# Perceiver block: the context product of batches 2 to 14 as seven half products instead of eight

## The chip, the core and the metric

One Trainium2 chip, one core. The time is the device time of one execution of the kernel, in microseconds (us). The engines are TensorE (PE in the profile; its weight loads are PEld), VectorE (DVE), ScalarE (ACT), GpSimd (POOL) and SyncE (SP, which only issues DMAs here). All tensors are float32.

## The reference

Sixteen batches of 128 tokens with 512 features pass through three layers. Only the first is touched by the change:

```python
def _L0_xattn_ref(hidden_states, visual_hidden_state):
    scores = jnp.einsum('bld,bvd->blv', hidden_states, visual_hidden_state)
    probs = jax.nn.softmax(scores, axis=-1)
    return jnp.einsum('blv,bvd->bld', probs, visual_hidden_state)
...
x = x + _L0_xattn_ref(_layernorm(x, axis=-1), ctx_1024)
x = x + _L0_attn_ref(_layernorm(x, axis=-1), ...)
x = x + _L0_ffn_ref(_layernorm(x, axis=-1), ...)
```

`ctx_1024` holds 2048 rows of 512 features for each batch. The "context product" is the second einsum: 128 x 2048 weights times 2048 x 512 context rows. The second layer is causal self-attention with 16 heads of 32 (its query, key and value weights are two factors, multiplied out once at the start), the third picks 2 of 8 low-rank experts for each batch.

## The kernel before

**Tiling.** A batch is 128 tokens on 128 partitions, or its transpose. The context is handled in four quarters of 512 rows (`v` = 0 to 3); the quarter comes twice from memory, once transposed (`ctxT`, for the scores) and once as rows (`ctx`, for the product), 1 MB each, four buffers each. `score` computes one quarter's scores, transposed, with 16 matmuls of 128x128x128 into a PSUM bank `psc`; `keep_score` copies them into the tile `sc` (ScalarE) and keeps a running maximum `mx` (VectorE). `turn_max`, `most`, `spread` turn that maximum into one value per token, spread over all partitions. `less` subtracts it (VectorE, one 128x512 instruction for each quarter), `power` takes the exponential (ScalarE), `sums` adds up the 16 tiles of the batch (VectorE). `attend` is the context product of one quarter: four matmuls with 128 weights columns and 512 moving columns, all 16 of the batch accumulating in one PSUM bank `av`. `x1_of` divides by the sum and adds the residual in one VectorE instruction that reads `av` from PSUM, and starts the next layer norm (`moments`: two VectorE instructions, then the reciprocal root `rs` as two small GpSimd instructions; `rows`: the normalized rows `h`; `turn`: a 32x32 transposition on VectorE and two DMAs through memory that give `hT`).

**One iteration of the main loop** (`b` = 0 to 13) works on four batches at once: self-attention of batch `b`, softmax and context product of `a = b + 1`, scores of `s = b + 2`, and the expert layer of `l = b - 1`. On TensorE its order is: tr_m (the transposed maximum of `a`), q, spread, k, v (projections of `b`), attend(a,0), compare (the 16 heads' scores `pss`), attend(a,1), lg (the expert logits), attend(a,2), den (the sum of the weights), attend(a,3), score(s,0), mid (experts, first factor), score(s,1), score(s,2), ffn (experts, second factor), y (the heads times v, from `pT`), score(s,3), o (the product with Wc). `mid` is written with 64 columns of the array for each of the two experts, side by side; `y` with 32 columns for each of four heads, `compare` with 32 rows for each of four heads.

VectorE in the same iteration: nm, diag (for `spread`), x2 and its norm, the four `less`, `h` and `turn` of layer 3, rotation of q and k (`rotate`: a shuffle, a product with the cosines; GpSimd does the product with the sines; `rotated` adds the two), `sums`, the router's `shares`, four groups of mask and maximum (`powers`), the choice of experts (`choose`), x1 and its norm, ten transpositions of 32 rows into `pT` (`turn_probs`), and the maxima `mx` of the next scores. GpSimd: `rs` of each norm, the token order for v, the residual of layer 3, the two products with the sines, four divisions of the probabilities (`divided`), three indirect DMAs (`fetch`), and the output's DMA.

**What sets the order.** Every instruction is issued through a wrapper that keeps the program order on its engine, so each engine works through a list written out by hand, and waits where an input or a buffer isn't there. Tiles come from pools with a fixed number of buffers in turn (`p1`: 1, `p2`: 2, `p3`: 3, `p4`: 4); a new tile waits until the reader of the one it replaces is done. The eight PSUM banks: 2 for scores (`ps_sc`), 1 for the context product (`ps_av`), 5 for all else (`ps_acc`). The DMAs of SP stand in one list too.

After the loop, batches 14 and 15 are finished by a list of their own; in it GpSimd adds up the sums of batch 15. In the profile nearly every instruction carries line 101, that of the wrapper, so rows are told apart by their tiles.

Of the kernel before, what the change touches and what calls it, by code (L numbers as in the profile page):

```python
# [11 lines left out]
F32 = mybir.dt.float32  # L12
# [3 lines left out]
ALU = mybir.AluOpType  # L16
# [50 lines left out]
def perceiver_block(ctx: ExitStack, tc: tile.TileContext, io: dict, out: bass.AP):  # L67
# [5 lines left out]
    p3 = ctx.enter_context(tc.tile_pool(name="p3", bufs=3))  # L73
    p4 = ctx.enter_context(tc.tile_pool(name="p4", bufs=4))
    ps_sc = ctx.enter_context(tc.tile_pool(name="ps_sc", bufs=2, space=PSUM))
    ps_av = ctx.enter_context(tc.tile_pool(name="ps_av", bufs=1, space=PSUM))
    ps_acc = ctx.enter_context(tc.tile_pool(name="ps_acc", bufs=5, space=PSUM))

    dram = ctx.enter_context(tc.tile_pool(name="dram", bufs=2, space=bass.MemoryType.DRAM))

# [25 lines left out]
    def bank(of, tag, name):  # L106
        return of.tile([P, 512], F32, tag=tag, name=name)
# [124 lines left out]
            cts[b, v] = t  # L232

    norms, hTs = {}, {}
    scs, mxs, psc, parts, dens, rdens, avs, spreads, trs = ({} for _ in range(9))
    x1s, x2s, projected, partners, turned_qk, values, hTvs = ({} for _ in range(7))
    atts, ys, yTs, os_, routes, mids, ffns = ({} for _ in range(7))
# [19 lines left out]

    def keep_score(b, v):
        if v == 0:
            scs[b] = p2.tile([P, VC, 4, S], F32, tag="sc", name=f"sc_{b}")  # L260
            mxs[b] = p1.tile([P, 4, S], F32, tag="mx", name=f"mx_{b}")
        sc, mx, ps = scs[b], mxs[b], psc.pop((b, v))
        act.copy(sc[:, v], ps)
        if v:
            dve.tensor_tensor(mx, ps, mx if v > 1 else sc[:, 0], ALU.max)
        if v == VC - 1:
            dve.tensor_tensor(mx[:, :2], mx[:, :2], mx[:, 2:], ALU.max)
            dve.tensor_tensor(mx[:, 0], mx[:, 0], mx[:, 1], ALU.max)
# [20 lines left out]
    def less(b, v):  # L289
        sc = scs[b]  # L290
        dve.tensor_tensor(
            sc[:, v], sc[:, v], spreads[b][:, None, :S].to_broadcast([P, 4, S]), ALU.add
        )

    def power(b, v):
        act.activation(scs[b][:, v], scs[b][:, v], AF.Exp)

    def sums(b, by=dve):
        sc = scs[b]
        t = p1.tile([P, 4, S], F32, tag="sums", name=f"sums_{b}")  # L300
        for v in range(1, VC):
            by.tensor_tensor(t, sc[:, v], t if v > 1 else sc[:, 0], ALU.add)
        part = p2.tile([P, S], F32, tag="part", name=f"part_{b}")
        by.tensor_tensor(t[:, :2], t[:, :2], t[:, 2:], ALU.add)
        by.tensor_tensor(part, t[:, 0], t[:, 1], ALU.add)
        parts[b] = part

    def attend(b, v):
        sc, ct = scs[b], cts.pop((b, v))
        if v == 0:  # L310
            avs[b] = bank(ps_av, "av", f"av_{b}")
        for j in range(4):
            matmul(
                avs[b], sc[:, v, j, :], ct[:, j, :],
                start=(v == 0 and j == 0), stop=(v == VC - 1 and j == 3),
            )
# [7 lines left out]
        dve.reciprocal(rdens[b], dens.pop(b)[:, :1])  # L324

    def x1_of(b):
        x1s[b] = p2.tile([P, D], F32, tag="x1", name=f"x1_{b}")
        dve.scalar_tensor_tensor(x1s[b], avs.pop(b), rdens.pop(b), xs.pop(b), ALU.mult, ALU.add)
        norms[2, b] = Norm(x1s[b], f"2_{b}", mixed=b in (0, B - 1), hT=(p1, "hT2")).moments()


# [12 lines left out]

    def rotate(b, n, by=pool):
        ps = projected.pop((n, b))
        partner = p1.tile([P, HC, S], F32, tag=f"{n}P", name=f"{n}P_{b}")
        dve.stream_shuffle(partner.rearrange("p c t -> p (c t)"), ps, PARTNERS)
        t = p1.tile([P, HC, S], F32, tag=f"{n}T", name=f"{n}T_{b}")
        dve.tensor_tensor(  # L350
            t, ps.rearrange("p (c t) -> p c t", c=HC),
            cst[:, None, C_COS : C_COS + S].to_broadcast([P, HC, S]), ALU.mult,
        )
        by.tensor_tensor(
            partner, partner, cst[:, None, C_SIN : C_SIN + S].to_broadcast([P, HC, S]), ALU.mult
        )
        turned_qk[n, b], partners[n, b] = t, partner
# [17 lines left out]
        projected["v", b] = ps  # L375

    def keep_v(b):
        values[b] = p2.tile([P, D], F32, tag="vv", name=f"vv_{b}")
        act.copy(values[b], projected.pop(("v", b)))

    def compare(b):
        qT, kT = turned_qk.pop(("q", b)), turned_qk.pop(("k", b))
        pss = [bank(ps_acc, "acc", f"pss_{b}_{j}") for j in range(4)]
        for c in range(HC):
            for j, ps in enumerate(pss):
                of = slice(j * DH, (j + 1) * DH)
                matmul(
                    ps[:, c * S : (c + 1) * S], qT[of, c, :], kT[of, c, :], start=True, stop=True
                )
        atts[b] = (  # L390
            p1.tile([P, H, S], F32, tag="att", name=f"att_{b}"),
            p2.tile([P, H], F32, tag="nmx", name=f"nmx_{b}"),
            p2.tile([P, H], F32, tag="sm", name=f"sm_{b}"),
            p2.tile([P, H], F32, tag="rsm", name=f"rsm_{b}"),
            pss,
        )
# [119 lines left out]
    def fetch(b):  # L516
        blocks, picked, ex = chosen[b]
        spare = b == B - 1
        each = (p2 if spare else p1).tile(
            [P, TOP, KC * R], F32, tag="sc" if spare else "each", name=f"each_{b}"  # L520
        )
        for i in range(TOP):
            pool.indirect_dma_start(
                each[:, i, :], None, io["A"],
                bass.IndirectOffsetOnAxis(ap=blocks[:, i : i + 1], axis=0),
            )
        wb = p2.tile([P, D], F32, tag="wb", name=f"wb_{b}")
        pool.indirect_dma_start(
            wb, None, io["BT"], bass.IndirectOffsetOnAxis(ap=picked, axis=0)
        )  # L530
        routes[b] = each, wb
# [26 lines left out]
    def first_joined(b):  # L558
        acc, v0 = bank(ps_acc, "acc", f"o0_{b}"), state["v0"]
        for c in range(KC):  # L560
            matmul(acc[:1, :], v0[:, c : c + 1], w["c"][:, c, :], start=(c == 0), stop=(c == KC - 1))
        row = p1.tile([1, D], F32, tag="sums", name=f"row_{b}")
        dve.tensor_tensor(row, acc[:1, :], x1s[b][:1, :], ALU.add)
        state["h"] = Norm(row, f"row_{b}", 1, "mx", mixed=True).moments()

# [128 lines left out]
    for b in range(B - 2):  # L694
        l, a, s = b - 1, b + 1, b + 2
        if b:
            turn_max(a)
            project(b, "q", [0])
            most(a)
            x2_of(l)  # L700
            spread(a)
            project(b, "q", [1, 2, 3])
            order_tokens(b)
            less(a, 0)
            power(a, 0)
            rows(3, l)
            turn(3, l)
            less(a, 1)
            power(a, 1)
            residual(l)  # L710
            load_x(s + 1)
            load_turned(s, 2)
            less(a, 2)
            power(a, 2)
        else:
            project(b, "q")
        rotate(b, "q")
        project(b, "k")
        if b:
            less(a, 3)  # L720
            power(a, 3)
            load_turned(s, 3)
        rotated(b, "q")
        rotate(b, "k")
        project_v(b)
        keep_v(b)
        rotated(b, "k")
        attend(a, 0)
        load_ctx(a + 1, 0)
        compare(b)  # L730
        if b:
            sums(a)
            shares(l)
        powers(b, 0)
        attend(a, 1)
        load_ctx(a + 1, 1)
        powers(b, 1)
        if b:
            logit(l)
            choose(l)  # L740
        divided(b, 0)
        if b:
            fetch(l)
        attend(a, 2)
        powers(b, 2)
        divided(b, 1)
        whole(a)
        portion(a)
        powers(b, 3)
        divided(b, 2)  # L750
        if b:
            gate(l)
        load_ctx(a + 1, 2)
        attend(a, 3)
        divided(b, 3)
        x1_of(a)
        score(s, 0)
        turn_probs(b, 0)
        rows(2, a)
        turn(2, a)  # L760
        keep_score(s, 0)
        if b:
            middle(l)
        for i in (1, 2):
            turn_probs(b, i)
        score(s, 1)
        turn_probs(b, 3)
        keep_score(s, 1)
        load_ctx(a + 1, 3)
        score(s, 2)  # L770
        if b:
            widen(l)
            end(l)
        load_turned(s + 1, 0)
        heads(b)
        keep_heads(b)
        keep_score(s, 2)
        score(s, 3)
        if s + 1 < B:
            norm1(s + 1)  # L780
        load_turned(s + 1, 1)
        if s + 1 < B:
            rows(1, s + 1)
            turn(1, s + 1)
        keep_score(s, 3)
        join(b)

# [156 lines left out]
```

## Time and profile before

| what | value |
|---|---|
| time, median of 3 runs | 812.87 us (811.56 to 814.71) |
| profiled execution, its own time | 812.89 us |
| its span, first to last instruction | 811.1 us |
| granted TensorE clock | 0.995 |
| VectorE busy, each 48 us from 108 to 684 | 36.5 to 37.0 us |
| ScalarE busy, the same | 13.1 to 13.4 us |
| GpSimd busy, the same | 14.5 us |
| DMA, mean busy share of 16 engines there | 0.62 to 0.64 |

A row of the timeline reads: start (us), duration (us), engine, line, operation, output<-inputs, shape, and how many instructions were merged into the row; in brackets the idle time ahead of it and what ended it. A float32 matmul counts as two records. A row of the page's groups has the total busy time and the mean of one instruction in ns.

### The profile page before, as it was taken

The page shows a single profiled execution, that of the slowest core. Times are in us where ns is not written, and L with a number is a line of the kernel's source. Part 1 is how long each engine was busy: PE and PEld are TensorE (multiplying, and loading weights), DVE is VectorE, ACT ScalarE, POOL GpSimd, SP SyncE. Part 2 cuts the span into 40 slices and gives each one's busy share as a digit, 9 for nine tenths or more (in the row PEclk, how much of TensorE's full clock was granted, in tenths as well). Part 3 has the DMA queues.
Part 4 walks back from the last instruction along what each step waited for, and adds up shares of the span by engine and source line. Part 5 has one row for each costly group of instructions (what it writes and reads, how often), then busy time and mean ns, then how long its engine had stood idle before and what let it go on. Part 6 is the DMA issues. An engine that isn't in the chain of part 4 may idle for free.

```text
span 811.1 us, 14245 instructions
## 1 busy us (share of the span) xinstructions
PE 793.7 (98%) x5506; PEld 570.6 (70%) x5506; DVE 581.7 (72%) x1289; ACT 223.6 (28%) x731; POOL 233.6 (29%) x295
## 2 busy tenths in 40 slices
PE   8999999999999999999999999999999999999985
PEld 8946785858677586867858686785868768586743
DVE  1446777787887778778777877877787777767673
ACT  1222323132142313214231321423132141313341
POOL 2001224133232403323240332324123232305333
PEclk9999999999999999999999999999999999999998
DMA  9989557567565856646585674658566565720001
GB/s 353 389 314 407 223 202 295 221 246 271 179 228 203 288 221 241 269 179 218 211 298 220 227 277 166 230 210 306 216 224 265 197 213 212 296 93 27 27 27 65
DMA packets 57971, 181.61 MB, mean 224 GB/s; under 512 B 5504, under 2 KB 27392, under 8 KB 41520
## 3 DMA queue, kind: packets, MB, share of 16 engines
q1 hardware_dynamic: 53760, 168.38, 55.9%
q0 software_dynamic: 4000, 12.26, 4.0%
q8 instruction: 43, 0.70, 0.3%
q14 instruction: 24, 0.20, 0.1%
q10 hardware_dynamic: 144, 0.07, 0.0%
HBM read 165.48 MB, written 15.20 MB: 223 GB/s over the span
## 4 chain that ended last, share of the span: by engine, by line
PE 96%; DVE 2%; DMA 1%; issue 0%; ACT 0%; POOL 0%; DVEq 0%; ACTq 0%
PE psc L101 29%; PE av L101 28%; PE q L101 7%; PE k L101 7%; PE o L101 7%; PE v L101 6%; PE pss L101 2%; PE mid L101 2%; PE ffn L101 2%; PE y L101 2%; PE spread L101 1%; PE tr L101 0%; PE tr_p L101 0%; DVE h L101 0%; DMA each<-in_A_dram,g_blocks 0%
## 5 line engine op out<-in xcount | busy, mean ns | idle before, releaser
L101 PEld LDWEIGHTS psc<-hT,ctxT 128*128 128x128 f32 x2048 | 234.7, 193 | 12.8 <-issue 9.1
L101 PE MATMUL psc<-hT,ctxT 128*128 128x128 f32 x2048 | 240.2, 277 | 0.7 <-ACT hT L101 0.7
L101 PE MATMUL av<-ctx,sc 128*128 128x512 f32 x512 | 232.9, 600 | 0.0
L101 PEld LDWEIGHTS av<-ctx,sc 128*128 128x128 f32 x512 | 93.6, 190 | 102.1 <-issue 100.3
L101 ACT ACTIVATE att<-att,nmx 128x128 f32<-128x128 f32 x256 | 99.2, 389 | 116.9 <-DVE nmx L101 114.6
L101 POOL TENSOR_TENSOR att<-att,rsm 128x512 f32<-128x512 f32 x60 | 61.2, 1041 | 166.3 <-DVE rsm L101 166.0
L101 DVE STREAM_TRANSPOSE pT<-att 32x512 f32<-32x512 f32 x140 | 98.3, 702 | 12.2 <-POOL att L101 10.3
L101 ACT COPY sc<-psc 128x512 f32<-128x512 f32 x64 | 37.6, 587 | 159.0 <-PE psc L101 159.0
L101 ACT ACTIVATE sc<-sc 128x512 f32<-128x512 f32 x64 | 39.7, 631 | 134.9 <-DVE sc L101 134.9
L101 POOL TENSOR_SCALAR rs<-mv 128x1 f32<-128x1 f32 x48 | 10.8, 226 | 185.4 <-DVE mv L101 183.6
L101 PEld LDWEIGHTS q<-hT,w_q 128*128 128x128 f32 x512 | 59.6, 192 | 4.1 <-issue 4.0
L101 PE MATMUL q<-hT,w_q 128*128 128x128 f32 x512 | 62.2, 275 | 0.0
L101 PE MATMUL k<-hT,w_k 128*128 128x128 f32 x512 | 59.8, 275 | 0.0
L101 PEld LDWEIGHTS k<-hT,w_k 128*128 128x128 f32 x512 | 58.5, 192 | 0.0
L101 PE MATMUL o<-w_c,yT 128*128 128x512 f32 x128 | 57.9, 594 | 0.0
L101 PE MATMUL v<-w_v,hTv 128*128 128x512 f32 x128 | 57.7, 593 | 0.0
L101 DVE TENSOR_TENSOR att<-pss,cst 128x512 f32<-128x512 f32 x64 | 43.3, 677 | 18.1 <-PE pss L101 18.1
L101 DVE TENSOR_SCALAR h<-x,mv,rs 128x512 f32<-128x512 f32 x48 | 33.0, 688 | 27.1 <-POOL rs L101 27.1
L101 POOL DMA_DIRECT2D out_dram<-x x14 | 9.2, 659 | 136.7 <-DVE x L101 136.7
L101 ACT ACTIVATION_READ_ACCUMULATOR att<-att,nmx 128x1 f32 x256 | 47.8, 187 | 0.0
L101 DVE TENSOR_REDUCE nmx<-att 128x4 f32<-128x512 f32 x64 | 43.9, 686 | 2.2
L101 DVE TENSOR_TENSOR mx<-psc,mx 128x512 f32<-128x512 f32 x32 | 21.6, 675 | 30.7 <-ACT sc L101 30.7
(132 smaller groups left out, 830.8 us busy)
## 6 DMA issues: line engine op xcount, KB each, us to landing
ctxT<-in_ctxT_dram SPq DMA_DIRECT2D x64, 1024.0 KB
ctx<-in_ctx_dram SPq DMA_DIRECT2D x64, 1024.0 KB
d<-turn SPq DMA_DIRECT2D x42, 256.0 KB
hT<-d SPq DMA_DIRECT2D x42, 256.0 KB
x<-in_x_dram SPq DMA_DIRECT2D x16, 256.0 KB
out_dram<-x POOLq DMA_DIRECT2D x14, 256.0 KB, 5.4
down_q<-in_Wq_downT_dram SPq DMA_DIRECT2D x2, 1024.0 KB
down_k<-in_Wk_downT_dram SPq DMA_DIRECT2D x2, 1024.0 KB
```

What stands on the lines that cost most here:

```text
L101: return lambda *args, **kwargs: tc.keep_in_program_order(issue(*args, **kwargs))
```

## The change

For batches 2 to 14 the context product is computed by Strassen's scheme in the form with 7 products: tokens, context rows and features are each cut into two halves (64 tokens, 2 of the 4 row tiles of a quarter, 256 features). The scheme needs sums of halves of both factors ahead of the products, and sums of products behind them.

- `context_halves`: four 128x512 subtractions of context halves for each quarter, on GpSimd, three into a new tile `more` (3 buffers), one in place. Quarters 0, 1, 2 of batch `a + 1` are issued in the iteration of `a`: after `x1_of(a)`, after `score(s, 1)`, and at the end ahead of `keep_score(s, 3)`. Quarter 3 of `a` is issued in its own iteration after `attend(a, 0)`.
- `token_halves`: four 128x512 additions and subtractions of the exponentials on VectorE, once for each batch, into a tile `blocks`, ahead of the rotation of q.
- `attend_halves`: for each quarter 14 matmuls with 64 weight columns and 256 moving columns instead of four with 128 and 512; two neighbours write the low and the high 64 partitions of a bank. Two banks for each batch.
- `attended`: the products are put together with three ScalarE copies and five VectorE additions; then the division and residual read the result from SBUF.
- Order: the four `less` and `power` stand together ahead of `rows(3, l)`; `portion(a)` stands behind `powers(b, 3)`.
- Buffers: `ps_av` 2 banks, `ps_acc` 4; two of the four `compare` banks come from `ps_sc`. To make room, `sc`, `part`, `vv`, `wb` have one buffer instead of two, q and k share the tile of the partners, and some rarely used tiles take the place of others.

```diff
-    ps_av = ctx.enter_context(tc.tile_pool(name="ps_av", bufs=1, space=PSUM))
-    ps_acc = ctx.enter_context(tc.tile_pool(name="ps_acc", bufs=5, space=PSUM))
+    ps_av = ctx.enter_context(tc.tile_pool(name="ps_av", bufs=2, space=PSUM))
+    ps_acc = ctx.enter_context(tc.tile_pool(name="ps_acc", bufs=4, space=PSUM))
...
+    def context_halves(b, v, by=pool):
+        if not by_halves(b):
+            return
+        ct = cts[b, v]
+        b11, b12, b21, b22 = (ct[:, 2 * k : 2 * k + 2, n * HD : (n + 1) * HD] for k in (0, 1) for n in (0, 1))
+        more = p3.tile([P, 3, 2, HD], F32, tag="more", name=f"more_{b}_{v}")
+        by.tensor_tensor(more[:, 1], b22, b12, ALU.subtract)
+        by.tensor_tensor(b12, b12, b11, ALU.subtract)
+        by.tensor_tensor(more[:, 0], b22, b12, ALU.subtract)
+        by.tensor_tensor(more[:, 2], b21, more[:, 0], ALU.subtract)
+        mores[b, v] = more
+
+    def token_halves(b):
+        sc = scs[b]
+        a11, a12, a21, a22 = (
+            sc[:, :, 2 * k : 2 * k + 2, m * HT : (m + 1) * HT] for m in (0, 1) for k in (0, 1)
+        )
+        t = p1.tile([P, 4, VC, 2, HT], F32, tag="blocks", name=f"blocks_{b}")
+        dve.tensor_tensor(t[:, 0], a21, a22, ALU.add)
+        dve.tensor_tensor(t[:, 1], t[:, 0], a11, ALU.subtract)
+        dve.tensor_tensor(t[:, 2], a11, a21, ALU.subtract)
+        dve.tensor_tensor(t[:, 3], a12, t[:, 1], ALU.subtract)
+        halves_of[b] = t
+
+    def attend_halves(b, v):
...
+        for k in range(2):
+            for at, cols, ps, tokens, features in (
+                (low, left, one, sc[:, v, k, low], ct[:, k, left]),
+                (high, left, one, t[:, 1, v, k], more[:, 0, k]),
+                (low, left, two, sc[:, v, 2 + k, low], ct[:, 2 + k, left]),
+                (high, left, two, sc[:, v, 2 + k, high], more[:, 2, k]),
+                (low, right, two, t[:, 3, v, k], ct[:, 2 + k, right]),
+                (high, right, two, t[:, 0, v, k], ct[:, k, right]),
+            ):
+                matmul(
+                    ps[at, cols], tokens, features,
+                    start=(v == 0 and k == 0 and cols == left),
+                    stop=(v == VC - 1 and k == 1 and cols == right),
+                )
+        for k, at in enumerate((low, high)):
+            matmul(one[at, right], t[:, 2, v, k], more[:, 1, k], start=False, stop=(v == VC - 1))
+
+    def attended(b):
...
+        act.copy(first, one[:, :HD])
+        act.copy(moved[HT:], one[:HT].rearrange("p (n d) -> p n d", n=2))
+        dve.tensor_tensor(
+            e, first[:, None, :].to_broadcast([P, 2, HD]),
+            two.rearrange("p (n d) -> p n d", n=2), ALU.add,
+        )
+        act.copy(moved[:HT, 0], e[HT:, 1])
+        dve.tensor_tensor(moved[HT:, 1], one[HT:, HD:], moved[HT:, 1], ALU.add)
+        dve.tensor_tensor(moved[HT:, 0], moved[HT:, 0], moved[HT:, 1], ALU.add)
+        dve.tensor_tensor(
+            e[HT:], e[HT:], moved[HT:, :1].to_broadcast([HT, 2, HD]), ALU.add
+        )
+        dve.tensor_tensor(e[:HT, 1], e[:HT, 1], moved[:HT, 0], ALU.add)
+        return x1s[b]
...
-            less(a, 0)
-            power(a, 0)
+            for v in range(VC):
+                less(a, v)
+                power(a, v)
             rows(3, l)
             turn(3, l)
...
             load_turned(s, 2)
+            if by_halves(a):
+                token_halves(a)
...
         load_ctx(a + 1, 0)
+        context_halves(a, 3)
         compare(b)
...
+        powers(b, 3)
         portion(a)
-        powers(b, 3)
...
         x1_of(a)
+        context_halves(a + 1, 0)
         score(s, 0)
...
         score(s, 1)
+        context_halves(a + 1, 1)
...
+        context_halves(a + 1, 2)
         keep_score(s, 3)
         join(b)
```

More of the change, by code (lines that the diff above doesn't have):

```diff
@@ L234, in perceiver_block @@
     norms, hTs = {}, {}
+    mores, halves_of = {}, {}
     scs, mxs, psc, parts, dens, rdens, avs, spreads, trs = ({} for _ in range(9))
@@ L259, in keep_score @@
         if v == 0:
-            scs[b] = p2.tile([P, VC, 4, S], F32, tag="sc", name=f"sc_{b}")
+            scs[b] = p1.tile([P, VC, 4, S], F32, tag="blocks" if b == 1 else "sc", name=f"sc_{b}")
             mxs[b] = p1.tile([P, 4, S], F32, tag="mx", name=f"mx_{b}")
@@ L302, in sums @@
             by.tensor_tensor(t, sc[:, v], t if v > 1 else sc[:, 0], ALU.add)
-        part = p2.tile([P, S], F32, tag="part", name=f"part_{b}")
+        part = p1.tile([P, S], F32, tag="part", name=f"part_{b}")
         by.tensor_tensor(t[:, :2], t[:, :2], t[:, 2:], ALU.add)
@@ L306, in sums, with by_halves @@
         parts[b] = part
+    HT, HD = S // 2, D // 2
+    def by_halves(b):
+        return 1 < b < B - 1
+    def context_halves(b, v, by=pool):
[9 more added lines that the diff above has]
+        mores[b, v] = more
@@ new lines, in attend_halves @@
+    def attend_halves(b, v):
+        sc, ct, more, t = scs[b], cts.pop((b, v)), mores.pop((b, v)), halves_of[b]
+        if v == 0:
+            avs[b] = [bank(ps_av, "av", f"av_{b}_{i}") for i in range(2)]
+        one, two = avs[b]
+        low, high = slice(0, HT), slice(HT, S)
+        left, right = slice(0, HD), slice(HD, D)
+        for k in range(2):
[14 more added lines that the diff above has]
+            matmul(one[at, right], t[:, 2, v, k], more[:, 1, k], start=False, stop=(v == VC - 1))
@@ new lines, in attended @@
+    def attended(b):
+        one, two = avs.pop(b)
+        x1s[b] = p2.tile([P, D], F32, tag="x1", name=f"x1_{b}")
+        e = x1s[b].rearrange("p (n d) -> p n d", n=2)
+        first = p1.tile([P, HD], F32, tag="first", name=f"first_{b}")
+        moved = p1.tile([P, 2, HD], F32, tag="moved", name=f"moved_{b}")
+        act.copy(first, one[:, :HD])
[12 more added lines that the diff above has]
+        return x1s[b]
@@ L308, in attend @@
     def attend(b, v):
+        if by_halves(b):
+            return attend_halves(b, v)
         sc, ct = scs[b], cts.pop((b, v))
@@ L326, in x1_of @@
     def x1_of(b):
-        x1s[b] = p2.tile([P, D], F32, tag="x1", name=f"x1_{b}")
-        dve.scalar_tensor_tensor(x1s[b], avs.pop(b), rdens.pop(b), xs.pop(b), ALU.mult, ALU.add)
+        if by_halves(b):
+            of = attended(b)
+        else:
+            of = avs.pop(b)
+            x1s[b] = p2.tile([P, D], F32, tag="x1", name=f"x1_{b}")
+        dve.scalar_tensor_tensor(x1s[b], of, rdens.pop(b), xs.pop(b), ALU.mult, ALU.add)
         norms[2, b] = Norm(x1s[b], f"2_{b}", mixed=b in (0, B - 1), hT=(p1, "hT2")).moments()
@@ L346, in rotate @@
         ps = projected.pop((n, b))
-        partner = p1.tile([P, HC, S], F32, tag=f"{n}P", name=f"{n}P_{b}")
+        partner = p1.tile([P, HC, S], F32, tag="partner", name=f"{n}P_{b}")
         dve.stream_shuffle(partner.rearrange("p c t -> p (c t)"), ps, PARTNERS)
@@ L377, in keep_v @@
     def keep_v(b):
-        values[b] = p2.tile([P, D], F32, tag="vv", name=f"vv_{b}")
+        values[b] = p1.tile([P, D], F32, tag="vv", name=f"vv_{b}")
         act.copy(values[b], projected.pop(("v", b)))
@@ L382, in compare @@
         qT, kT = turned_qk.pop(("q", b)), turned_qk.pop(("k", b))
-        pss = [bank(ps_acc, "acc", f"pss_{b}_{j}") for j in range(4)]
+        pss = [
+            bank(*((ps_sc, "sc") if j < 2 else (ps_acc, "acc")), f"pss_{b}_{j}") for j in range(4)
+        ]
         for c in range(HC):
@@ L518, in fetch @@
         spare = b == B - 1
-        each = (p2 if spare else p1).tile(
-            [P, TOP, KC * R], F32, tag="sc" if spare else "each", name=f"each_{b}"
+        each = p1.tile(
+            [P, TOP, KC * R], F32, tag="blocks" if spare else "each", name=f"each_{b}"
         )
@@ L526, in fetch @@
             )
-        wb = p2.tile([P, D], F32, tag="wb", name=f"wb_{b}")
+        wb = p1.tile([P, D], F32, tag="sums" if spare else "wb", name=f"wb_{b}")
         pool.indirect_dma_start(
@@ L561, in first_joined @@
             matmul(acc[:1, :], v0[:, c : c + 1], w["c"][:, c, :], start=(c == 0), stop=(c == KC - 1))
-        row = p1.tile([1, D], F32, tag="sums", name=f"row_{b}")
+        row = p1.tile([1, D], F32, tag="moved", name=f"row_{b}")
         dve.tensor_tensor(row, acc[:1, :], x1s[b][:1, :], ALU.add)
@@ L703, in perceiver_block @@
             order_tokens(b)
-            less(a, 0)
-            power(a, 0)
+            for v in range(VC):
+                less(a, v)
+                power(a, v)
             rows(3, l)
             turn(3, l)
-            less(a, 1)
-            power(a, 1)
             residual(l)
@@ L712, in perceiver_block @@
             load_turned(s, 2)
-            less(a, 2)
-            power(a, 2)
+            if by_halves(a):
+                token_halves(a)
         else:
@@ L719, in perceiver_block @@
         if b:
-            less(a, 3)
-            power(a, 3)
             load_turned(s, 3)
```

## The prediction

> **What bounds the kernel now.** I read the engine rows of the page first, then the chain, the stretches of 48 us, and the timeline of one batch.
>
> ```profile
> PE 793.7 (98%) x5506; PEld 570.6 (70%) x5506; DVE 581.7 (72%) x1289; ACT 223.6 (28%) x731; POOL 233.6 (29%) x295
> ...
> PE 96%; DVE 2%; DMA 1%; issue 0%; ACT 0%; POOL 0%; DVEq 0%; ACTq 0%
> ```
>
> TensorE has 98% of the span and 96% of the chain, and in each 48 us stretch from 108 to 684 it is busy 48.00. Timeline, TensorE, one batch (start, us):
>
> ```profile
> 301.31 0.27 PE L101 MATMUL tr_m<-cst,mx 128*128 128x128 f32 x1
> ...
> 312.30 3.60 PE L101 MATMUL av<-ctx,sc 128*128 128x512 f32 x8
> 315.82 1.17 PE L101 MATMUL pss<-kT,qT 32*128 32x128 f32 x32
> ...
> 331.44 1.09 PE L101 MATMUL mid<-hT,each 128*64 128x128 f32 x16
> 332.47 7.41 PE L101 MATMUL psc<-hT,ctxT 128*128 128x128 f32 x64
> ...
> 340.67 1.08 PE L101 MATMUL y<-pT,vv 128*32 128x128 f32 x32
> ...
> 348.79 0.27 PE L101 MATMUL tr_m<-cst,mx 128*128 128x128 f32 x1
> ```
>
> The period is 348.79 - 301.31 = 47.48. How close is the next engine? VectorE in the same batch:
>
> ```profile
> 332.65 6.44 DVE L101 STREAM_TRANSPOSE pT<-att 32x512 f32<-32x512 f32 x9
> 339.12 0.69 DVE L101 TENSOR_TENSOR mx<-psc,sc 128x512 f32<-128x512 f32 x1
> ```
>
> The matmuls y need all of pT. VectorE ends pT at 339.09, TensorE starts y at 340.67: slack 1.58. So there is a second loop: tr_m, VectorE's list up to pT, then y, the last score and the product with Wc (8.12 from y to the next tr_m), tr_m. With t = 0 at tr_m, pT is done at 37.8, and the loop needs 45.9 of the 47.5.
>
> GpSimd idles 71%, but how do it and VectorE get on? Three places (the first two fences from the timeline near the end, the third in mid kernel):
>
> ```profile
> 740.16 1.26 POOL L101 TENSOR_TENSOR sums<-sc 128x512 f32<-128x512 f32 x1
> 740.23 1.74 DVE L101 TENSOR_TENSOR kT<-kT,kP 128x512 f32<-128x512 f32 x1 [0.81 <-POOL kP L101]
> ...
> 741.50 1.60 POOL L101 TENSOR_TENSOR sums<-sc,sums 128x512 f32<-128x512 f32 x1
> ```
>
> ```profile
> 799.82 1.52 POOL L101 TENSOR_TENSOR x<-x,h 128x512 f32<-128x512 f32 x1
> 799.87 1.92 DVE L101 TENSOR_SCALAR h<-x,mv,rs 128x512 f32<-128x512 f32 x1 [1.94 <-POOL rs L101]
> ```
>
> ```profile
> 305.66 1.27 POOL L101 TENSOR_TENSOR x<-x,h 128x512 f32<-128x512 f32 x1 [0.37 <-DVE h L101]
> 306.25 1.24 DVE L101 TENSOR_TENSOR sc<-sc,spread 128x512 f32<-128x512 f32 x2
> ```
>
> kT+kP takes 0.69 elsewhere; started inside a GpSimd sum it took 1.74 and ended 0.55 after GpSimd did. GpSimd's next sum, started inside it, took 1.60 instead of 1.26. The normalization h (0.55 alone) took 1.92. But sc+spread, one input in PSUM, keeps 0.62 each beside GpSimd. So an addition of two SBUF tensors, or h, and a GpSimd sum run one after the other.
>
> **The product on TensorE.** Removed per batch and quarter: four 128x512 matmuls, 315.82 - 312.30 = 3.52, 0.88 each. Added: seven pairs with 256 columns. A full 128-column matmul takes (339.72 - 332.47)/32 = 0.227; between that and 0.88, 256 columns take about 0.444. Is a pair as fast as one? mid is four pairs 64 wide: 332.47 - 331.44 = 1.03, against 4 x 0.227 = 0.91, so 0.12 for the change of shape and no more. A rule speaks against it: the Trainium skill, "TensorE: Matmul & The Clock Gate", "Measured speedup vs the span model", has three column tiles (32 wide, 512 columns) reach only 2.38 times one. By that 79%, 14 x 0.444/1.59 = 3.91 a quarter, 52 quarters lose 20 us; by the row 7 x 0.444 + 0.12 = 3.23, 52 x 0.29 = 15 us gained. I take the row. No row has 64 wide with different moving operands; y has it 32 wide (0.25 a group of four), which points the same way. If pairs did not overlap: 6.2, +2.7 a quarter.
>
> **VectorE's additions** (batches 2 to 14: 13 iterations). Token halves: four 128x512 at 0.66 to 0.72, 2.7. Joining: 0.68 + 0.42 + 0.42 + 0.69 + 0.42 = 2.65, from the 128x512 and 128x256 rows (a 64-partition row is not in the trace; the free size has set the time in all rows). ACT's three copies, 0.40 + 0.59 + 0.40, stand ahead of the next score's copy, which has 3 us of room; but the first is waited for, 0.35, as it queues behind the last exponentials. Without GpSimd the list runs so: four subtractions of the maximum 2.4 to 4.9, h and turn to 6.2, token halves to 8.9, q rotated by 11.6 and k by 14.4 (each waits 0.8 for GpSimd's product), sums and shares to 17.7, four rounds of scores and the choice to 27.3, joined, normed 31.9, h and turn 34.2, pT 40.6. Old waits (pss 0.72, lg 0.64, den 0.39, att 0.79) vanish on the way, the sum of the new is +2.8. The loop is 40.6 + 0.1 + 8.12 = 48.8, above 47.48 by 1.35; TensorE's saving is lost in waiting for pT. Even with no waits at all 37.8 - 5.1 + 5.35 = 38.0 is just where the saving could be kept.
>
> **GpSimd's additions**: 4 sums a quarter at 1.27 (rows qP, x), 5.1; 20.3 a batch, 14.5 to 35 of 47: it has the room. But its queue sets when they run, and there they meet VectorE:
> - Quarter 3 starts when attend(a,0) frees its tile (14.2), just when VectorE starts its sums, all SBUF. They alternate: GpSimd 1.27, sum 0.55, and so on; shares end at 22.5 instead of 17.7, +4.7. TensorE waits for lg behind it.
> - Joining meets the three divisions: two small adds each wait out a division, +1.3.
> - Quarter 0 starts on the same signal as h of batch a; at 799.82 and at 754.30 GpSimd was first: +1.2. Quarter 1 lies beside transposes, which ran at 0.71 beside GpSimd: 0.
> - The residual meets the first token half: +0.5.
> - Quarter 2 is issued behind the last norm's rs: h again, then the 256- and 128-wide folds of mx each behind a sum. The rows show only 128x512 forms delayed; by these alone the folds cost 0. The Trainium skill, "SBUF — State Buffer", "Who interferes with whom", says that any VectorE instruction with two SBUF inputs is held for the whole GpSimd instruction, whatever its size; by it tr_m comes 10.7 after pT instead of 8.1, +2.6. I take the rule: 12 x 2.6 = 31 us hang on it.
>
> Sum per iteration: 1.35 + 4.7 + 1.3 + 1.2 + 0.5 + 2.6 = 11.6; the first wait takes some of the next, I keep 11.1: a period of 58.6. Twelve such iterations 133; the 13th has no quarters to prepare (11.1 - 1.2 - 2.6 = 7.3), iteration 0 only quarters 0 to 2 with room before them (2). 133 + 7 + 2 = 142 on the profiled execution's 812.89 (span 811.1, and 1.8 around it; the median 812.87 is the same): 955.
>
> **The rest**, at nothing: fetch's DMAs move with the choice and land (4.8 after issue) before pT, which is later still; turn of h comes 1.2 later, its two DMAs and the ctxT loads behind it on SP have over 5 us until their readers. One buffer less for sc, part, vv, wb, partner: each reader is done an iteration before, or in order on the same engine. PSUM: four acc banks; every one asked for was freed by a VectorE or ACT read at least one step before. If that cover failed: one late bank is at most a 0.7 read. TensorE's idle stretches (3.2 before lg, 4 before y) could lower its clock; the last stretch, with 15% idle, was granted 0.96. Cost 0 to 2 a batch; I take 0.
>
> **Rivals.**
> A, as above: 955, own range 920 to 985. Chance 0.70.
> B, the meetings happen only for 128x512 sums and h in mid batch (4.7 + 1.2 + 1.35 = 7.2): 12 x 7.2 + 7 = 906. 0.12.
> C, GpSimd and VectorE hardly meet; only the lengthened VectorE list counts: 13 x 1.35 = 17.5, 830. Against it, the two fences. 0.07.
> D, the other side: TensorE stays the bound, 797. It decides if pT is done by 38.1 (TensorE's new period 46.3 less 8.2): VectorE's list would have to be 2.5 shorter than the rows make it, and all the meetings harmless. 0.05.
> E, pairs do not overlap: 52 x 2.7 = 140 on TensorE, and part of A's waits on top: 985. Rows mid and y speak against. 0.06.
>
> **Numbers.** Predicted 955. The range 870 to 990 holds A, B and most of E. Within 0.5% (about what a measurement can tell) is 809 to 817: between C and D, 0.02; faster 0.05, slower 0.93.
>
> **What would show it.** A period near 58 with TensorE at about 80% busy; waits of lg for VectorE's g_part (3 us) and of y for pT (4 us); seven pairs a quarter in about 3.2; the VectorE sums at 1.8 each, h at 1.8; GpSimd near 35 a batch. If the sums stay at 0.69, C is right; if TensorE is still at 98%, D (short quarters) or E (quarters of 6.2). Wrong also if GpSimd's sums on these slices are not 1.27.

## The result, and the profile after

The changed kernel takes 956.41 us (953.99 to 958.19, 4 runs) against 813.79 us for the kernel before, measured beside it: 1.1755 times, 95% interval 1.1716 to 1.1793. Predicted were 955, in a range of 870 to 990. The profiled execution has a span of 954.9 us.

The page after, engine row and chain:

```profile
PE 838.0 (88%) x6546; PEld 626.0 (66%) x6546; DVE 763.4 (80%) x1406; ACT 237.0 (25%) x770; POOL 514.3 (54%) x503
...
DVE 57%; PE 27%; POOL 5%; ACT 5%; issue 4%; DMA 1%; POOLq 0%; DVEq 0%; ACTq 0%
```

TensorE was 96% of the chain and is 27% now; VectorE is 57%. The 88% of "busy" TensorE contains matmuls that run slowly, as the next views show. Timeline of TensorE in one iteration (start, us; the brackets are waits):

```profile
345.55 0.33 PE L101 MATMUL tr_m<-cst,mx 128*128 128x128 f32 x1 [0.43 <-DVE mx L101]
...
367.71 0.57 PE L101 MATMUL lg<-g_part,ones 128*128 128x8 f32 x2 [2.85 <-DVE g_part L101]
...
393.17 1.94 PE L101 MATMUL y<-pT,vv 128*32 128x128 f32 x32 [3.94 <-DVE pT L101]
395.03 5.33 PE L101 MATMUL psc<-hT,ctxT 128*128 128x128 f32 x32
...
404.37 0.33 PE L101 MATMUL tr_m<-cst,mx 128*128 128x128 f32 x1 [0.57 <-DVE mx L101]
```

The period is 404.37 - 345.55 = 58.82; over the twelve full iterations it is 57.96 to 59.31, 58.68 in the mean, where the prediction had 58.6. The waits named there are in place: 2.85 us of lg for VectorE's g_part, and of y for pT (3.94 here; 2.28 to 5.46 over the twelve). Taken at nothing there, and there all the same: behind that wait y takes 1.94 instead of 1.08 and the score 5.33 instead of 3.84. (In three of the twelve, those with 2.28 to 2.35 idle, y still takes 1.08 and the score 5.46.) The profile's rows by stretch say why. Each has the stretch, its length, the busy time of PE, PEld, DVE, ACT and POOL, then the granted clock of TensorE, the DMA share and GB/s:

```profile
392.00:396.00 4.00, 2.83 (x36) 2.35 (x37) 2.39 (x4) 0.83 (x2) 3.43 (x4) 0.50 1.06 403
396.00:400.00 4.00, 4.00 (x29) 4.00 (x28) 2.68 (x4) 0.24 (x1) 2.03 (x3) 0.73 0.98 377
```

TensorE was granted half its clock while y and the first part of the score ran. The same happens behind the wait of lg (0.57 from 367 to 371), where it costs nothing: y waits for pT afterwards in any case.

VectorE and GpSimd in the same iteration:

```profile
360.37 1.75 DVE L101 TENSOR_TENSOR sums<-sc 128x512 f32<-128x512 f32 x1
362.16 3.32 DVE L101 TENSOR_TENSOR sums<-sc,sums 128x512 f32<-128x512 f32 x2
...
384.41 1.49 DVE L101 TENSOR_SCALAR h<-x,mv,rs 128x512 f32<-128x512 f32 x1 [0.42 <-POOL rs L101]
...
401.75 2.56 DVE L101 TENSOR_TENSOR mx<-mx 128x256 f32<-128x256 f32 x2
```

```profile
360.08 1.49 POOL L101 TENSOR_TENSOR more<-ctx 128x512 f32<-128x512 f32 x1 [0.35 <-PE av L101]
...
384.36 1.26 POOL L101 TENSOR_TENSOR more<-ctx 128x512 f32<-128x512 f32 x1
```

The same instructions of VectorE in the kernel before:

```profile
313.67 1.49 DVE L101 TENSOR_TENSOR sums<-sc,sums 128x512 f32<-128x512 f32 x2
...
331.33 0.55 DVE L101 TENSOR_SCALAR h<-x,mv,rs 128x512 f32<-128x512 f32 x1 [0.16 <-POOL rs L101]
...
347.39 0.75 DVE L101 TENSOR_TENSOR mx<-mx 128x256 f32<-128x256 f32 x2
```

The sums and GpSimd's quarter 3 go in turn: the first of VectorE's additions ends at 362.12, after the GpSimd instruction that it met (361.57), and two more take 3.32 instead of 1.49. The two folds of mx take 2.56 instead of 0.75. h starts 0.05 after GpSimd's first subtraction of quarter 0 and ends 0.28 after it.

### The profile page after: what moved, and what is told of

It reads as the page before. It is cut to its first block, busy times and chain, and to the rows that moved or that the text cites. A ratio compares the mean times of both kernels' runs of the same rounds, so it can differ in the third digit from the quotient of the medians.

```text
span 954.9 us, 16829 instructions
## 1 busy us (share of the span) xinstructions
PE 838.0 (88%) x6546; PEld 626.0 (66%) x6546; DVE 763.4 (80%) x1406; ACT 237.0 (25%) x770; POOL 514.3 (54%) x503
## 4 chain that ended last, share of the span: by engine, by line
DVE 57%; PE 27%; POOL 5%; ACT 5%; issue 4%; DMA 1%; POOLq 0%; DVEq 0%; ACTq 0%
DVE pT L101 9%; DVE sums L101 9%; PE av L101 8%; PE psc L101 8%; DVE mx L101 4%; DVE blocks L101 4%; DVE h L101 4%; DVE x L101 4%; ACT att L101 3%; DVE moved L101 3%; DVE st L101 3%; DVE sc L101 3%; DVE nmx L101 3%; PE y L101 3%; DVE turn L101 2%
## 5 line engine op out<-in xcount | busy, mean ns | idle before, releaser
L101 PE MATMUL av<-ctx,sc 128*64 128x256 f32 (+1 forms) x512 | 168.4, 461 | 0.0
L101 POOL TENSOR_TENSOR more<-ctx 128x512 f32<-128x512 f32 x104 | 138.7, 1334 | 8.2 <-PE av L101 4.2
L101 PEld LDWEIGHTS av<-ctx,sc 128*64 128x64 f32 (+1 forms) x512 | 76.6, 159 | 60.8 <-issue 39.9
L101 PE MATMUL av<-more,blocks 128*64 128x256 f32 x416 | 106.3, 418 | 0.0
L101 DVE TENSOR_SCALAR h<-x,mv,rs 128x512 f32<-128x512 f32 x48 | 54.2, 1129 | 26.3 <-POOL rs L101 26.3
L101 POOL TENSOR_TENSOR ctx<-ctx 128x512 f32<-128x512 f32 x52 | 72.1, 1387 | 4.1
L101 POOL TENSOR_TENSOR more<-ctx,more 128x512 f32<-128x512 f32 x52 | 70.9, 1364 | 4.1
L101 PE MATMUL av<-ctx,blocks 128*64 128x256 f32 x416 | 70.5, 421 | 0.0
L101 PE MATMUL av<-more,sc 128*64 128x256 f32 x208 | 70.1, 423 | 0.0
L101 PE MATMUL y<-pT,vv 128*32 128x128 f32 x512 | 25.0, 357 | 47.0 <-DVE pT L101 47.0
```

The source lines that it names most:

```text
L101: return lambda *args, **kwargs: tc.keep_in_program_order(issue(*args, **kwargs))
```

## The experiments

Each leaves the rest of the changed kernel as it is. M is the prediction's theory (VectorE and GpSimd block each other in certain instructions), L its rival (nothing blocks; the added instructions themselves are what takes time), K the addition that the slow y suggested: an idle stretch lowers TensorE's clock. Several leave out sums that the scheme needs, so they compute something else and serve for their times only. Periods are from one tr_m to the next.

**No GpSimd subtractions.**

```diff
-        if not by_halves(b):
+        if not by_halves(b) or True:
             return
...
+        if more is None:
+            m0, m1, m2 = ct[:, :2, HD:], ct[:, 2:, :HD], ct[:, 2:, HD:]
```

> Leaves out GpSimd's 208 subtractions of context halves; the products take plain slices of the context instead. M (GpSimd and VectorE block each other): what is left is VectorE's longer list, pT done near 40.6 after tr_m, a period of 48.8, in all 813 + 13 x 1.35 = 831 us (825 to 840); the sums at 0.69 to 0.75 each, h at 0.55. L (no blocking; the lengthening comes from the added VectorE and ScalarE work itself): VectorE keeps all its instructions, so above 935 us.

Measured: 878.75 us. L is out: 78 us of the 143 go with GpSimd's subtractions. But the 831 was missed by 48. VectorE, then TensorE, in one iteration (tr_m at 424.48):

```profile
439.26 0.69 DVE L101 TENSOR_TENSOR sums<-sc 128x512 f32<-128x512 f32 x1
...
453.64 1.78 DVE L101 TENSOR_TENSOR moved<-moved 64x256 f32<-64x256 f32 x1
```

```profile
467.20 1.93 PE L101 MATMUL y<-pT,vv 128*32 128x128 f32 x32 [3.48 <-DVE pT L101]
469.06 4.58 PE L101 MATMUL psc<-hT,ctxT 128*128 128x128 f32 x32
```

The sums are back at 0.69. The joining still meets GpSimd's divisions (1.78 instead of 0.43), and the first token half GpSimd's residual (1.23 instead of 0.69): these meetings are with work that GpSimd had before, and the expectation forgot them, 1.9 together. pT is done 42.65 after tr_m; less 1.9 that is 40.75, the prediction's list (40.6). The other miss is K: y and the score take 1.6 longer. 48.8 + 1.9 + 1.6 = 52.3, and the period is 52.43. (The twelve periods run from 50.8 to 53.6; in the two shortest TensorE kept its full clock.)

**The sums ahead of quarter 3**, the same work.

```diff
-        context_halves(a, 3)
         compare(b)
         if b:
             sums(a)
+        if by_halves(a):
+            hold(parts[a][:, :1])
+        context_halves(a, 3)
```

(`hold` copies one column on GpSimd, so that its queue waits for the result.)

> Same work; GpSimd starts quarter 3 only after VectorE's sums (a one-column copy of their result stands ahead of it). M: the sums run undisturbed, 4.2 to 4.7 us less for each of 13 iterations, 895 to 910 us. L: GpSimd's work is only later, 956 us, within 5.

Measured: 930.64 us, 26 less, where M expected at least 46. The sums ran undisturbed (g_part ends 18.1 after tr_m instead of 22.0), but about half of the gain was lost again elsewhere:

```profile
469.96 1.15 DVE L101 TENSOR_SCALAR nmx<-nmx 128x4 f32<-128x4 f32 x1
```

Quarter 3 now lies beside the attention's maxima, and there the four-column nmx, 0.17 before, waits out a GpSimd subtraction. And since TensorE is no longer held at lg, its idle time ahead of y grows to 5.86, and it stays slow behind that.

**Quarter 2 left out.**

```diff
-        if not by_halves(b):
+        if not by_halves(b) or v == 2:
```

> Leaves out the subtractions of quarter 2 (52 of 208), which run at the end of an iteration beside h and the folds of mx. M alone: 2.6 us less for each of 12 iterations, 925 us. M with a lowered TensorE clock as a second wait of the same length: tr_m then waits for the product with Wc instead, which ended only 0.4 to 0.9 ahead of the folds; 0.5 to 1 us each, 944 to 951 us. L: 0 to 4 us less.

Measured: 949.81 us. h and the folds of mx are no longer delayed, and yet only 6.6 us are gained, because y (1.93) and the score (5.20) remain slow and end almost when the folds did. M alone, with 925, is out.

**TensorE kept at work ahead of y.**

```diff
+        if by_halves(a):
+            warm = bank(ps_acc, "acc", f"warm_{b}")
+            for i in range(12):
+                matmul(warm[:, :P], ones, ones, start=True, stop=True)
         heads(b)
```

> Same work, plus 12 matmuls 128x128x128 of ones into a spare bank ahead of y, 2.7 us of the 2.3 to 5.9 us in which TensorE waits for pT. K (the idle stretch lowers TensorE's clock: y takes 1.94 instead of 1.01, the score behind it 5.3 instead of 3.7): both are back at full speed, but tr_m then waits for the folds of mx, which were only 0.4 to 0.9 late: 944 to 952 us. If the clock is no cause: y and the score stay slow or the time stays 956.

Measured: 949.24 us (946.98 and 951.50, so about as much as the step before). TensorE:

```profile
451.29 1.08 PE L101 MATMUL y<-pT,vv 128*32 128x128 f32 x32 [1.09 <-DVE pT L101]
452.30 3.84 PE L101 MATMUL psc<-hT,ctxT 128*128 128x128 f32 x32
...
461.63 0.33 PE L101 MATMUL tr_m<-cst,mx 128*128 128x128 f32 x1 [2.05 <-DVE mx L101]
```

The granted clock from 451 to 456 is 1.00. With about 1.1 idle (up to 1.4) instead of 2.3 to 5.5, y and the score are at full speed in ten of the twelve full iterations; in the other two, 2.78 were left idle, and both were slow. K holds. y to tr_m takes 10.34 instead of 11.20: the 0.86 are those that y itself lost, for ScalarE's copy of y stands ahead of the copy that VectorE's maxima and folds wait for. What the score saves turns up as the wait of tr_m for the folds, 2.05.

**Both.**

> e3 (the subtractions of quarter 2 left out) and the 12 matmuls together. K with M: two waits of nearly the same length stand side by side at the end of an iteration, and only with both gone is the gain there: tr_m 8.2 after pT, 2.5 to 3 us less for each of 12 iterations, 918 to 928 us. If each were a cost of its own, the gains of e3 (6) and e4 would add up: about 942.

Measured: 936.71 us, between the two expectations. TensorE is done with ffn 1.7 earlier than in the step before, pT comes at the same time, and so 2.78 us mostly remain idle behind the 12 matmuls. Five of twelve periods are 55.8, what K with M expects; the others are 57.4 or more, with a slow score (5.01 to 5.47). Where the clock held, the gain is more than the sum of the two. Four of the five fast iterations had the same 2.8 idle as the slow ones: what decides whether the clock falls after such a stretch is not shown here.

**Without VectorE's and ScalarE's additions**: no token halves, no joining; GpSimd's subtractions stay.

```diff
-            if by_halves(a):
-                token_halves(a)
...
-            of = attended(b)
+            one, of = avs.pop(b)
```

> Leaves out what the change added to VectorE and ScalarE (token halves and the joining; the products take plain scores, one bank is read as the result), keeps GpSimd's 208 subtractions. M: pT at 47.6 - 2.7 - 0.5 - 2.65 - 1.6 - 0.35 = 39.8, the end of the iteration still 11.3: a period near 51, 860 us (850 to 875). L: VectorE's list is that of before and GpSimd has room, 800 to 815 us.

Measured: 852.64 us, in M's range; L, with VectorE's list of before, is out. TensorE waits little for pT here (0 to 0.7), runs y and the score at full speed, and shows h and the folds by themselves:

```profile
456.65 1.08 PE L101 MATMUL y<-pT,vv 128*32 128x128 f32 x32
...
467.00 0.33 PE L101 MATMUL tr_m<-cst,mx 128*128 128x128 f32 x1 [2.06 <-DVE mx L101]
```

10.35 from y to tr_m instead of 8.12: quarter 2, by delaying h and the folds, costs 2.2 where y and the score are not slow.

**Only the half products**: neither GpSimd's nor VectorE's sums. The half products, the new order and the tighter buffers and banks are all that differs from the kernel before.

> Only the 14 half matmuls a quarter are left of the change: no context halves, no token halves, no joining (plain slices, one bank read as the result). The recorded prediction's TensorE term, with the pair now read as 0.428 and the quarter as 3.17 instead of 3.52: 52 x 0.35 = 18 us less than before, 795 us (792 to 800), TensorE at 98%. If the pairs brought something else with them (weights, banks, the shorter PSUM rota): 813 or more.

Measured: 810.56 us (8 runs), 0.9957 times before, 0.9935 to 0.9980. TensorE, this kernel, then the kernel before:

```profile
318.46 0.39 PE L101 MATMUL lg<-g_part,ones 128*128 128x8 f32 x2
318.78 3.24 PE L101 MATMUL av<-ctx,sc 128*64 128x256 f32 x28
321.95 0.38 PE L101 MATMUL den<-ones,part 128*128 128x1 f32 x2
```

```profile
320.47 0.28 PE L101 MATMUL lg<-g_part,ones 128*128 128x8 f32 x2
320.61 3.68 PE L101 MATMUL av<-ctx,sc 128*128 128x512 f32 x8
324.12 0.28 PE L101 MATMUL den<-ones,part 128*128 128x1 f32 x2
```

The quarter itself is 321.95 - 318.78 = 3.17, but lg ahead of it takes 0.32 instead of 0.14: the change of shape is paid on both sides. From lg to den the kernel before has 324.12 - 320.47 = 3.65, this one 3.49, 0.16 less. From v to mid, which holds all four quarters and their neighbours, it is 21.7 instead of 22.6: some 0.85 an iteration, 11 us in thirteen. But mid, now earlier, waits for the experts' DMA, so that in ten of the thirteen iterations 1.5 to 2.4 instead of 1.03 pass from mid to the next score, 8 us in all. Of the gain 3 us are left. The expectation took the bare quarter, and no wait. Since this kernel is no slower than the one before, the order, buffers and banks of the change are no cause of its loss.

**GpSimd as busy, but reading nothing.**

```diff
-        by.tensor_tensor(more[:, 1], b22, b12, ALU.subtract)
-        by.tensor_tensor(b12, b12, b11, ALU.subtract)
-        by.tensor_tensor(more[:, 0], b22, b12, ALU.subtract)
-        by.tensor_tensor(more[:, 2], b21, more[:, 0], ALU.subtract)
+        for i in range(4):
+            by.memset(more, 0.0)
```

> GpSimd's four subtractions of each quarter are replaced by four fills of the 1536-element tile (same place, about as long, 1.4 us each), so it is as busy but reads no SBUF; the products use zeros. M (VectorE's additions of two SBUF tensors wait for GpSimd's reads): the sums are back at 0.69 to 0.75, 880 to 900 us, near e1's 879; h may still wait if it meets writes too. If what counts is only that GpSimd is busy, or its queue: 945 us or more.

Measured: 905.77 us, 51 less than the changed kernel, 6 above M's range. VectorE, beside fills at 453.25, 473.66 and 488.13:

```profile
454.28 1.42 DVE L101 TENSOR_TENSOR sums<-sc,sums 128x512 f32<-128x512 f32 x2
...
458.18 0.79 DVE L101 TENSOR_SCALAR nmx<-nmx 128x4 f32<-128x4 f32 x1
...
473.73 1.58 DVE L101 TENSOR_SCALAR h<-x,mv,rs 128x512 f32<-128x512 f32 x1 [0.42 <-POOL rs L101]
...
491.48 0.75 DVE L101 TENSOR_TENSOR mx<-mx 128x256 f32<-128x256 f32 x2
```

Two kinds of meeting come apart. The sums and the folds, additions of two SBUF tensors, run free beside a GpSimd that only writes: it is GpSimd's reading that stops them. h and nmx, a tensor with scalars, wait all the same, which the expectation left open: with h's wait, pT is done at 43.7 after tr_m, where the first experiment had 42.65.

**All four quarters out of the way**: the gate of the sums, another behind h (quarter 0), another behind the folds (quarter 2).

```diff
         rows(2, a)
+        if by_halves(a + 1):
+            hold(norms[2, a].h[:, :1])
+        context_halves(a + 1, 0)
...
         keep_score(s, 3)
+        if by_halves(a + 1):
+            hold(mxs[s][:, 0, :1])
+        context_halves(a + 1, 2)
```

> Same work as the change; GpSimd waits, by one-column copies, until VectorE has its sums (quarter 3), its h (quarter 0) and the folds of mx (quarter 2) behind it. M: quarter 3 gains the 2.1 of e2, quarter 0 about 1.0; quarter 2 now runs at the start of the next iteration, in front of rs and beside diag, and costs 1.1 + 0.5 there, while the end stays bound by TensorE at its lowered clock: about 56 us an iteration, 918 to 932 us. If the gains of the gates simply added up (2.1 + 1.0 + 2.6): 882 us.

Measured: 910.12 us, a period of 54.7; better than expected, far from 882. The gates don't add up: quarter 2 now delays diag (1.12 instead of 0.29) and with it the spreading, 0.74 of TensorE, and the end stays bound by a slow y and score.

**The same, with TensorE kept at work ahead of y.**

> e9 with 26 matmuls of ones (5.9 us) in the idle stretch ahead of y. K with M: with folds and clock both out of the way the end shrinks from 10.3 to 8.3 after pT: about 54 us an iteration, 895 to 910 us. Without K: as e9.

Measured: 907.16 us (902.88 and 911.44), no clear gain over 910. y and the score were at full speed, and nine of thirteen periods are 54.3 to 54.4, but the filling got in the way itself. TensorE, then VectorE, in one of the four longer iterations, where the 26 matmuls ran from 483.48 to 489.45:

```profile
489.38 1.08 PE L101 MATMUL y<-pT,vv 128*32 128x128 f32 x32
```

```profile
483.95 2.86 DVE L101 STREAM_TRANSPOSE pT<-att 32x512 f32<-32x512 f32 x4
```

pT was done at 486.81, 2.57 before y could begin; in the nine shorter iterations it was 0.9. 26 matmuls were too many.

**With 14 matmuls of ones.**

> The same kernel with 14 matmuls of ones (some 3.2 us) instead of 26 ahead of y. With 26, y in the iteration from 441.50 began at 489.38, 2.57 after pT was done (486.81), because the filling itself still ran; with none, y waited 4.5 for pT and ran slowly. M with K: y starts within 0.2 of pT, the score at full speed (3.84), so 45.0 from tr_m to pT and 8.2 to 8.7 behind it give a period of 53.3 to 53.7, about 1 less than with 26: 892 to 900 us. If the filling wasn't in the way, or if the folds of mx and not y set the end (M without K): 905 to 912, with a wait of tr_m for the folds of 1 to 2.

Measured: 897.9 us (895.56 to 898.74), 1.103 times before (1.1008 to 1.1052), as M with K expects (the period came out 0.2 above, as pT is done at 45.7 and not 45.0). TensorE, in an iteration in which y still waits for pT:

```profile
747.83 1.08 PE L101 MATMUL y<-pT,vv 128*32 128x128 f32 x32 [1.81 <-DVE pT L101]
...
755.95 0.27 PE L101 MATMUL tr_m<-cst,mx 128*128 128x128 f32 x1
```

From y to tr_m are 755.95 - 747.83 = 8.12, what the kernel before has: neither clock nor folds are left there. Most periods are 53.9, and the 45.8 of it up to y are VectorE's list with its remaining meetings. That is 6.4 above the 47.5 of the kernel before. It is the fastest version that does all of the scheme's work, and beats neither the kernel before nor the half products alone.

## Why the prediction was right

The mechanism was right in the main, VectorE's loop with GpSimd's meetings in it; one cause, TensorE's clock, was named and then taken at nothing. That the sum came within 2 us is luck in part: single steps are off by up to 0.75 us an iteration, in both directions. By its steps:

- **The second loop** (tr_m, VectorE up to pT, y to tr_m) is what bounds: pT is done 47.6 after tr_m (47.8 in the working of 58.6). That VectorE's list alone, 40.6, gives away the whole saving: 40.75 by the first experiment, once its 1.9 of meetings with old GpSimd work are taken off.
- **The sums beside quarter 3**: g_part ends 22.0 after tr_m, 18.1 without GpSimd's subtractions: 3.95, predicted 4.7.
- **Joining** 1.6 (predicted 1.3: two small additions behind one division each; in fact one of them reads PSUM and keeps its 0.43, and the other takes 2.02 and ends after the last of two divisions), **residual** 0.55 (0.5), **h beside quarter 0** 0.93 (1.2).
- **The end of the iteration** was right by luck in part. Predicted were +2.6, with the Trainium skill's rule on two SBUF inputs ("SBUF — State Buffer", "Who interferes with whom") for the narrow folds, and 0 for TensorE's clock. Measured from y to tr_m are 11.2 in nine iterations, +3.1, and 10.35 in the three in which y kept its speed, +2.2. The rule holds: the folds, 256 and 128 elements wide, wait as the wide additions do, and h and the folds cost 2.2 at full clock. It names only GpSimd instructions that read SBUF, and so it is here: beside fills the folds took 0.75. But the clock, put at 0 to 2 and taken as 0, costs 2.0 to 2.2 by itself, as the step without quarter 2 shows. Of that, y's 0.86 come on top of the folds, and the score's share lies beside them. Leaving out either cause gained 7 us, not 31, so "12 x 2.6 = 31 us hang on it" was wrong: they hung on both.
- **TensorE's product**: the step "52 x 0.29 = 15 us gained" was mis-sized. The row was the right one for the pair (0.43 from the start of one to the next, 0.444 taken; by an estimate from the 2.38 in the Trainium skill, "TensorE: Matmul & The Clock Gate", "Measured speedup vs the span model", which is for 32-wide tiles, it would have been 0.56). But the change of shape costs 3.17 - 7 x 0.43 = 0.16 inside a quarter, where 0.12 was taken, and up to 0.18 at a neighbour, where nothing was. With the half products alone 11 us are gained and 3 reach the time. It did not matter to the sum since TensorE isn't the bound.
- **Iteration 0 and the 13th** were put at +2 and +7.3, and are +3.0 (68.56 against 65.53) and +7.3 (54.81).
- **Rival C** (830) was worked out too low: without any new meeting the first experiment, without GpSimd's subtractions, gives 879, since the old GpSimd work meets the new additions, and the clock falls.

Not tried: the subtractions put into the kernel before without the rest, and other homes for them than GpSimd.

## What to carry to other kernels

GpSimd idled 71% here and wasn't free to use. Before giving such an engine work, list what its neighbour runs at the moment when the queue will start that work. Price each meeting of a VectorE addition of two SBUF tensors with a GpSimd instruction that reads SBUF as a wait for that instruction's end. When one engine bounds at 98% and the next has 1.6 us of slack in a period of 47, a saving on the first can't pay for 5 us on the second: work out the second loop first. And when a wait is taken away and little is gained, look for one of the same length beside it before discarding the cause.

## What the runs showed that was not expected

- TensorE slows after a short idle stretch. Over all runs above, y and the score kept full speed whenever TensorE had idled up to 1.8 us ahead of y, and one or both were slow whenever it had idled more than 3.5 us; in between, from 2.2 to 3.5, they were slow in 22 of 27 iterations. A slow y takes up to 1.94 and a slow score up to 5.9. The mean granted clock of the profiled run is 0.932 here, 0.995 before.
- Instructions as small as 128x4 (nmx, 0.17) wait for the end of the GpSimd instruction that they meet: 1.15 beside subtractions, 0.79 beside fills.
- A change of the array's shape is paid by the neighbour too: lg, a matmul with 8 columns, holds TensorE for 0.32 between half products, 0.14 between full ones.
